# Two of eight products with B moved from VectorE to GpSimd in a state-space scan

## The chip, the cores and the metric

One NeuronCore of a Trainium2 chip runs the whole program. The metric is the device time of one execution in microseconds; of a kernel it is the median of its runs. Smaller is better. Engines are named TensorE (PE in the profile), VectorE (DVE), ScalarE (ACT), GpSimd (POOL) and SyncE (SP, which here only issues DMAs).

## The reference

The program is four layers on an image of 2 x 128 x 64 x 64 in fp32. The change touches the first layer only, two Mamba blocks over 4096 tokens of 128 channels. Cut to the recurrence:

```python
xz = x @ in_w.T
u, z = jnp.split(xz, 2, axis=-1)                 # 256 inner channels each
u = silu(causal_conv4(u) + conv_b)
dt, Bm, Cm = jnp.split(u @ xproj_w.T, [R, R + N], axis=-1)   # R = 8, N = 16
dt = softplus(dt @ dt_w.T + dt_b)
dA = exp(dt[..., None] * A)                      # token x 256 x 16
dBu = (dt * u)[..., None] * Bm[:, :, None, :]    # the product with B
def step(h, inp):                                # over the tokens
    dA_t, dBu_t, C_t = inp
    h = dA_t * h + dBu_t
    return h, einsum('bdn,bn->bd', h, C_t)       # the product with C, summed over n
y = (ys + u * ssm_D) * silu(z)                   # the gate
return y @ out_w.T                               # the mixer's output product
```

Around each block stand a layer norm, a residual, and a feed-forward part with a GELU. Layers 2 to 4 (two attentions over the image and a multi-scale attention) follow unchanged.

## The kernel before

**Chunks and steps.** The tokens go in 32 chunks of 512 (2 images x 2 blocks x 8). A chunk has 256 channels x 16 states = 4096 recurrences. They are done in eight steps, numbered 0 to 7: one step takes 32 channels and all 16 states as 128 partitions (4 groups of states, q, times 32 channels) by 4 states in the free dimension, a tile h of 128 x 4 x 512. For each step:

- `spread_dt` (line 373): four DMAs on SP copy 32 rows of dt into the four quarters of the tile dtb. `decay` (391): ScalarE takes exp(dt A) from dtb into da, a PSUM tile, four times a step.
- `spread_dtu` (380): a matmul with a selection matrix repeats 32 rows of dt * u four times down the partitions, into the PSUM tile pdu. There is one such buffer (pool l0bc), so the next spread waits until VectorE has read the last.
- `times_b` (385): VectorE multiplies bb (B, repeated down the partitions by DMA) with pdu, broadcast over the 4 states, into h. h is a ring of five buffers, taken in turn; the hidden layer of the feed-forward part, hid (452), takes one of the ring per chunk too.
- `scan` (398): VectorE runs four scans in place on h. After the fourth, GpSimd copies the last column into carry (409) and multiplies h by cb, that is C (410).
- `y_pair` (412): TensorE sums two steps over the states into py, 8 products, and so frees two h buffers.

**Order.** The order is written out by hand (`tc.manual_schedule`). Every engine works through its own queue in the order in which the program issues. A chunk has 32 slots, one for each scan; `slot` (542) issues in slot 4s: `spread_dt` for three steps ahead, `spread_dtu` for the next step, and in every second step the `y_pair` of the steps three and two before; then a scan and a decay; in slot 4s + 3 `times_b` for the next step; then what `background` (489) lists for the slot. That list holds the work of neighbouring chunks: for the next chunk n the input product (`pu_taps`, slots 0 to 5), `xproj`, `dtproj`, `soft_plus` and `dt_end` (13 to 18, the last a product on GpSimd giving dtu); for the chunk before, p, `y_out` and `gate` (slot 7; the gate is a product on GpSimd, line 433), `mix_out` on TensorE (slot 9, line 439), which reads the gated z; for p and r = i + 2 the layer norms (slots 12 to 29, with two small products on GpSimd, lines 274 and 279); for q = i - 2 the rest of the feed-forward part.

**The start.** Before chunk 0 the weights of layer 2's convolutions are folded by VectorE (`fold`, 190, slots 8 to 10 of the period -1), in raw, ulo and uhi tiles that live in the h ring, and written to DRAM from SP at once.

Of the kernel before, what the change touches and what calls it, by code (L numbers as in the profile page):

```python
# [6 lines left out]
F32 = mybir.dt.float32  # L7
AF = mybir.ActivationFunctionType
ALU = mybir.AluOpType
# [4 lines left out]
B, C, H, W = 2, 128, 64, 64  # L14
N = H * W
P = 128
CH = 512
# [50 lines left out]
def tile_conv_seq(ctx: ExitStack, tc, x, consts, vecs, wemb, wlay, wconv, wdt, wqkv, wsmall, wms, out):  # L68
    nc = tc.nc
# [46 lines left out]
    with tc.manual_schedule(), ExitStack() as s:  # L116
# [4 lines left out]
        sp = scans.enter_context(tc.tile_pool(name="l0s", bufs=1, side="right"))  # L121
        bc = scans.enter_context(tc.tile_pool(name="l0bc", bufs=1, space=PSUM, side="right"))
# [15 lines left out]
        def four(g):  # L138
            return fsel[:, g].rearrange("p q d -> p (q d)")
# [30 lines left out]
                nc.vector.tensor_tensor(u[:, k, :], cw[:, KC, :], cw[:, k, :], ALU.mult)  # L170
            wu.append(u), am.append(a)

        raws = []

        def load_rest():
            for which in range(3):
# [13 lines left out]
        def fold(which):  # L190

            g = [raws[which][:, :, k, :] for k in range(3)]
            lo, hi = (sp.tile([P, 3, 3, C], F32, name=n, tag="h", bufs=5) for n in ("ulo", "uhi"))
            tt, ts, stt = nc.vector.tensor_tensor, nc.vector.tensor_scalar, nc.vector.scalar_tensor_tensor
            tt(lo[:, 1], g[0], g[2], ALU.add)
            ts(lo[:, 1], lo[:, 1], -1.0 / 6, None, ALU.mult)
            stt(lo[:, 0], g[1], 1.0 / 6, lo[:, 1], ALU.mult, ALU.add)
            stt(lo[:, 1], g[1], -1.0 / 6, lo[:, 1], ALU.mult, ALU.add)
            stt(hi[:, 0], g[2], 4.0, g[0], ALU.mult, ALU.add)
            ts(hi[:, 0], hi[:, 0], 1.0 / 24, None, ALU.mult)  # L200
            stt(lo[:, 2], g[1], -1.0 / 12, hi[:, 0], ALU.mult, ALU.add)
            stt(hi[:, 0], g[1], 1.0 / 12, hi[:, 0], ALU.mult, ALU.add)
            ts(hi[:, 1], g[0], 0.25, None, ALU.mult)
            nc.vector.tensor_copy(hi[:, 2], g[2])
            for k, u in enumerate((lo, hi)):
                nc.sync.dma_start(ufold[which][:, 9 * k : 9 * k + 9, :], u.rearrange("p s y c -> p (s y) c"))


# [4 lines left out]
        NI, NST, NSL = len(items), 8, 32  # L213
        st = [{} for _ in items]
# [3 lines left out]
        def has(i):  # L218
            return 0 <= i < NI
# [153 lines left out]
        def spread_dt(g):  # L373
            i, s_ = divmod(g, NST)
            o = st[i]["dtb", s_] = sp.tile([P, CH], F32, name="dtb", tag="dtb", bufs=4)
            k = 32 * (s_ % 4)
            for q in range(4):
                nc.sync.dma_start(o[32 * q : 32 * q + 32, :], st[i]["dt"][k : k + 32, s_ // 4, :])

        def spread_dtu(g):  # L380
            i, s_ = divmod(g, NST)
            pdu = st[i]["pdu", s_] = bc.tile([P, CH], F32, name="pdu", tag="bc")
            nc.tensor.matmul(pdu, lhsT=four(s_ % 4), rhs=st[i]["dtu"][:, s_ // 4, :], start=True, stop=True)  # L383

        def times_b(g):
            i, s_ = divmod(g, NST)
            h = st[i]["h", s_] = sp.tile([P, 4, CH], F32, name="h", tag="h", bufs=5)
            pdu = st[i].pop(("pdu", s_))
            nc.vector.tensor_tensor(h, st[i]["bc", 0], pdu.unsqueeze(1).to_broadcast([P, 4, CH]), ALU.mult)  # L389
# [8 lines left out]
        def scan(t):  # L398
            g, m = divmod(t, 4)
            i, s_ = divmod(g, NST)  # L400
            j, gg = divmod(s_, 4)
            b, l, c = items[i]
            if (b, l) not in carries:
                carries[b, l] = sp.tile([P, NJ, 4, 4], F32, name="carry", tag="carry", bufs=2)
                nc.gpsimd.memset(carries[b, l], 0.0)
            h, da = st[i]["h", s_], st[i].pop(("da", s_, m))
            nc.vector.tensor_tensor_scan(h[:, m, :], da, h[:, m, :], carries[b, l][:, j, gg, m : m + 1], ALU.mult, ALU.add)  # L407
            if m == 3:
                nc.gpsimd.tensor_copy(carries[b, l][:, j, gg, :].unsqueeze(2), h[:, :, CH - 1 : CH])  # L409
                nc.gpsimd.tensor_tensor(h, h, st[i]["bc", 1], ALU.mult)  # L410

        def y_pair(g):

            i, s_ = divmod(g, NST)
            j, gg = divmod(s_, 4)
            if gg == 0:
                st[i]["py", j] = yp.tile([P, CH], F32, name="py", tag="y")
            py = st[i]["py", j]
            for m in range(4):
                for k in range(2):  # L420
                    r = 32 * (gg + k)
                    nc.tensor.matmul(  # L422
                        py[r : r + 32, :], lhsT=sel, rhs=st[i]["h", s_ + k][:, m, :], start=(m == 0), stop=(m == 3),
                        tile_position=(0, r),
                    )
# [63 lines left out]
        def background(i):  # L489

            todo = [[] for _ in range(NSL)]

            def at(t, f, *a):
                todo[t].append((f, a))

            n, p, q, r = i + 1, i - 1, i - 2, i + 2
            if has(q):
                at(3, gelu, q)
                at(6, ffn_down, q, (0, 1)), at(7, ffn_down, q, (2, 3)), at(9, ffn_add, q)
                at(11, out_mm, q), at(12, out_add, q)  # L500
            if has(p):
                at(7, y_out, p, 1), at(7, gate, p)
                at(9, mix_out, p), at(11, mix_add, p)
            if has(n):
                at(0, pu_taps, n, 0, (0, 1)), at(1, pu_taps, n, 0, (2, 3)), at(2, pu_out, n, 0)
                at(3, pu_taps, n, 1, (0, 1)), at(4, pu_taps, n, 1, (2, 3)), at(5, pu_out, n, 1)
                at(13, xproj, n), at(14, xproj_out, n), at(14, spread_bc, n, 0), at(22, spread_bc, n, 1)
                at(15, dtproj, n, 0), at(16, dtproj, n, 1), at(17, soft_plus, n), at(18, dt_end, n)
            if has(i):
                at(1, pz_mm, i, 0), at(3, pz_out, i, 0)  # L510
                at(5, pz_mm, i, 1), at(6, pz_out, i, 1)
            if has(i) or has(n):
                at(11, silu, i, n)
            if i == -1:
                at(1, load_rest), at(7, prepare, 1)
                for k in range(3):
                    at(8 + k, fold, k)
                at(19, spread_dtu, 0), at(26, times_b, 0)
            pair = [(k, second) for k, second in ((p, True), (r, False)) if has(k)]
            if has(r):  # L520
                at(10, embed, r), at(11, embed_out, r)
            w, m = {}, len(pair)
            for k, (it, second) in enumerate(pair):
                at(12 + 2 * k, ln_centre, w, k, it)
                at(13 + 2 * k, ln_square, w, k, it)
                at(27, ln_spread, w, k, m), at(28, ln_scale, w, k, it)
                at(29, ln_shift, w, k, it, second)
            if pair:
                at(17, ln_var, w, m), at(18, ln_eps, w, m), at(19, ln_rs, w, m), at(20, ln_newton, w, m), at(21, ln_step, w, m)
            if has(p):  # L530
                for f in range(4):
                    at(30 + f // 2, ffn_up, p, f)
            if has(i):
                at(24, y_out, i, 0)
            return todo
# [5 lines left out]
        NG, NT = NI * NST, NI * NSL  # L541
        def slot(i, todo, t_):
            t = i * NSL + t_
            g, m = divmod(t, 4)
            if m == 0 and 0 <= g + 3 < NG:
                spread_dt(g + 3)
            if m == 0 and 1 <= g + 1 < NG:
                spread_dtu(g + 1)
            if m == 0 and g % 2 == 1 and 0 <= g - 3 < NG:
                y_pair(g - 3)  # L550
            if 0 <= t < NT:
                scan(t)
            if 0 <= t + 4 < NT:
                decay(t + 4)
            if m == 3 and 1 <= g + 1 < NG:
                times_b(g + 1)
            for f, a in todo[t_]:
                f(*a)
        for i in range(-2, NI):
            todo = background(i)  # L560
            for t_ in range(NSL):
                slot(i, todo, t_)
        todo = background(NI)
        for t_ in range(8):
            slot(NI, todo, t_)
# [331 lines left out]
        sp = s.enter_context(tc.tile_pool(name="ats", bufs=1, reuse_waits="tile"))  # L897
        psa = s.enter_context(tc.tile_pool(name="atpa", bufs=2, reuse_waits="tile", space=PSUM))
        psm = s.enter_context(tc.tile_pool(name="atpm", bufs=1, reuse_waits="tile", space=PSUM))
        for now in range(NALL + LAG + 10):  # L900
            r, u = divmod(now, NU)
# [71 lines left out]
    with ExitStack() as s, tc.manual_schedule():  # L973
        sp = s.enter_context(tc.tile_pool(name="mss", bufs=1, reuse_waits="tile"))
# [60 lines left out]
        st = [{} for _ in items]  # L1035
# [433 lines left out]
```

## Time and profile before

| | |
|---|---|
| median of 3 runs | 5001.07 us (5000.54 to 5005.86) |
| the profiled execution's own time | 5004.69 us |
| its span in the trace | 5002.9 us |
| scan stage | about the first 2,100 us of the span |
| VectorE busy, of 200 us from 1000 to 1200 | 182.16 us |
| TensorE busy, same stretch | 182.66 us |
| GpSimd busy, same stretch | 139.03 us |
| products with B on VectorE | 256, mean 2272 ns |
| products with C on GpSimd | 256, mean 4535 ns |
| spreads of dtu on TensorE | 256 products, 512 matmul records |

The profile gives busy time per engine, groups of equal instructions (line, engine, operation, output <- inputs, count, then busy us, mean ns, idle before them and what ended it), and a timeline. A timeline line has the start and the length in us, the engine, the line, the instruction, how many are merged, and in brackets the idle time before it with its releaser. An fp32 matmul leaves two records; L383 is a line of the kernel. SPq is the DMA queue of SP. All times count from the span's start.

### The profile page before, as it was taken

The numbers are of one execution on the slowest core, as the hardware profiler recorded it, in microseconds if no ns is written. First come the engines' busy times: TensorE is split into PE (matmuls) and PEld (weight loads), VectorE is DVE, ScalarE is ACT, GpSimd is POOL, SyncE is SP. The second block draws the span as 40 slices with busy tenths as digits, with TensorE's granted clock in tenths as the row PEclk, the third lists the DMA queues.
The fourth block names the chain that finished last, engine by engine and source line by source line (L and its number), as shares of the span: only waits on it lengthen the run. The fifth ranks groups of instructions, "written<-read, shape, count | busy, mean of one in ns | idle before, by whom it ended". The sixth has DMA issues, their size and how long they took to land. (4 is left out here: it accounts for less than half of the span.)

```text
span 5002.9 us, 48954 instructions
## 1 busy us (share of the span) xinstructions
PE 4661.3 (93%) x14797; PEld 2242.4 (45%) x14797; DVE 4024.6 (80%) x4283; ACT 2358.8 (47%) x3218; POOL 2337.5 (47%) x1974
## 2 busy tenths in 40 slices
PE   5889999999988899899999999999999999999997
PEld 1222222222222222366667766666666666333332
DVE  6999999999999999878886677767776775667776
ACT  4677777777777777522222222233333332323332
POOL 3777776766777777513332133333333332333331
PEclk8898889989999989899999999999999999999998
DMA  6333333322323333214444344434443443000000
GB/s 163 69 68 68 69 71 70 69 65 62 72 67 68 70 73 73 73 53 113 109 110 123 105 112 111 120 95 114 110 100 98 112 113 88 3 7 7 5 7 9
DMA packets 242343, 386.24 MB, mean 77 GB/s; under 512 B 88592, under 2 KB 88992, under 8 KB 233632
## 3 DMA queue, kind: packets, MB, share of 16 engines
q1 hardware_dynamic: 192928, 315.94, 26.0%
q10 hardware_dynamic: 49152, 67.17, 5.4%
q8 instruction: 118, 1.93, 0.2%
q14 instruction: 145, 1.19, 0.1%
HBM read 101.02 MB, written 13.37 MB: 23 GB/s over the span
## 5 line engine op out<-in xcount | busy, mean ns | idle before, releaser
L792 POOL COPY pt<-tr 32x512 f32<-32x512 f32 x1024 | 650.8, 636 | 1437.3 <-DVE tr L785 704.7
L407 DVE TENSOR_TENSOR_SCAN h<-da,carry,h 128x512 f32<-128x512 f32 x1024 | 1241.6, 1266 | 59.7 <-ACT da L396 30.7
L410 POOL TENSOR_TENSOR h<-h,cb 128x2048 f32<-128x2048 f32 x256 | 1160.9, 4535 | 21.0 <-POOL carry L409 0.4
L755 PE MATMUL pq<-k,q 128*128 128x512 f32 x2048 | 962.6, 593 | 7.0 <-DVE sc L760 7.0
L805 PE MATMUL po<-pt,vt 128*128 128x256 f32 x4096 | 965.7, 379 | 2.5 <-DMA pt<-tr 2.5
L770 ACT ACTIVATE sc<-sc,nm 128x2048 f32<-128x2048 f32 x256 | 510.6, 1995 | 912.8 <-DVE nm L766 701.6
L805 PEld LDWEIGHTS po<-pt,vt 128*128 128x128 f32 x4096 | 777.9, 190 | 294.8 <-issue 208.3
L760 DVE TENSOR_SCALAR_CACHE_REDUCE sc<-pq 128x1024 f32<-128x1024 f32 x512 | 625.1, 1222 | 315.6 <-PE pq L755 294.3
L396 ACT ACTIVATE da<-dtb,am 128x512 f32<-128x512 f32 x1024 | 681.5, 684 | 230.5 <-DVE h L407 207.9
L389 DVE TENSOR_TENSOR h<-bb,pdu 128x2048 f32<-128x2048 f32 x256 | 581.7, 2272 | 86.0 <-PE py L422 29.3
L785 DVE STREAM_TRANSPOSE tr<-sc 128x2048 f32<-128x2048 f32 x256 | 591.6, 2311 | 64.6 <-DMA pt<-tr 56.2
L422 PE MATMUL py<-h,sel 128*32 128x512 f32 x2048 | 511.0, 643 | 1.6 <-POOL h L410 1.6
L755 PEld LDWEIGHTS pq<-k,q 128*128 128x128 f32 x2048 | 382.9, 190 | 283.2 <-issue 247.2
L383 PE MATMUL pdu<-dtu,fsel 128*128 128x512 f32 x512 | 325.3, 721 | 117.0 <-DVE h L389 114.8
L422 PEld LDWEIGHTS py<-h,sel 128*32 128x32 f32 x2048 | 115.2, 117 | 415.0 <-issue 409.5
L310 PE MATMUL pu<-xn,wu 128*128 128x512 f32 x512 | 246.2, 614 | 2.6 <-ACT xn L300 1.7
L383 PEld LDWEIGHTS pdu<-dtu,fsel 128*128 128x128 f32 x512 | 95.9, 214 | 322.0 <-DVE h L389 199.5
L409 POOL COPY carry<-h 128x4 f32<-128x4 f32 x256 | 47.8, 187 | 394.5 <-DVE h L407 392.7
L1219 DVE TENSOR_TENSOR ov<-v,pw 128x2048 f32<-128x2048 f32 x64 | 146.2, 2285 | 62.1 <-PE pw L1212 62.1
L1153 PE MATMUL pqkv<-f,ws 128*128 128x512 f32 x384 | 188.2, 615 | 3.0 <-DVE prod L1170 2.3
L1223 POOL TENSOR_TENSOR ov<-ov 128x2048 f32<-128x2048 f32 x16 | 72.6, 4538 | 235.5 <-DVE ov L1219 235.5
L370 POOL TENSOR_TENSOR dtu<-dt,u 128x1024 f32<-128x1024 f32 x32 | 75.1, 2348 | 192.6 <-ACT dt L364 192.6
(259 smaller groups left out, 5266.6 us busy)
## 6 DMA issues: line engine op xcount, KB each, us to landing
pt<-tr SPq DMA_DIRECT2D x2048, 64.0 KB, 2.0
dtb<-dt SPq DMA_DIRECT2D x1024, 64.0 KB, 2.0
pt<-tr ACTq DMA_DIRECT2D x1024, 64.0 KB, 2.2
bb<-dr SPq DMA_DIRECT2D x128, 256.0 KB, 4.4
cb<-dr SPq DMA_DIRECT2D x128, 256.0 KB, 4.6
uw<-ufold SPq DMA_DIRECT2D x12, 576.0 KB, 4.3
uw<-dkept SPq DMA_DIRECT2D x20, 288.0 KB, 3.0
xt<-in_x SPq DMA_DIRECT2D x16, 256.0 KB, 4.6
```

What stands on the lines that cost most here:

```text
L383: nc.tensor.matmul(pdu, lhsT=four(s_ % 4), rhs=st[i]["dtu"][:, s_ // 4, :], start=True, stop=True)
L389: nc.vector.tensor_tensor(h, st[i]["bc", 0], pdu.unsqueeze(1).to_broadcast([P, 4, CH]), ALU.mult)
L396: nc.scalar.activation(da, st[i]["dtb", s_], AF.Exp, scale=am[items[i][1]][:, j, gg, m : m + 1])
L407: nc.vector.tensor_tensor_scan(h[:, m, :], da, h[:, m, :], carries[b, l][:, j, gg, m : m + 1], ALU.mult, ALU.add)
L410: nc.gpsimd.tensor_tensor(h, h, st[i]["bc", 1], ALU.mult)
L422: nc.tensor.matmul(py[r : r + 32, :], lhsT=sel, rhs=st[i]["h", s_ + k][:, m, :], start=(m == 0), stop=(m == 3), tile_position=(0, r),)
L755: nc.tensor.matmul(pq[:, i, :], lhsT=sta["q", r, grp][:, it * P : (it + 1) * P], rhs=sta["k"][:, at : at + CH], start=True, stop=True)
L760: nc.vector.tensor_scalar(dst, pq, 1.0, None, ALU.mult, ALU.max, accum_out=sta["mx"][:, c2 : c2 + 1])
L770: nc.scalar.activation(sc, sc, AF.Exp, bias=nm, scale=scale, accum_out=sm[:, hh : hh + 1])
L785: nc.vector.transpose(tr, sta.pop(("sc", r, blk, hh)).rearrange("p (t r f) -> p r t f", r=NB, f=32))
L792: nc.gpsimd.tensor_copy(dst, src)
L805: nc.tensor.matmul(sta["po", r, grp], lhsT=sta["vt"][:, jt, :], rhs=rhs, start=(jt == 0), stop=(jt == N // P - 1))
```

## The change

In every chunk, steps 3 and 5 (the fourth and the sixth) are taken out of `spread_dtu` and `times_b`. Instead SP copies their rows of dtu into an SBUF tile dub with four DMAs (`spread_pool`, in slots 0 and 5; dub has one buffer), and GpSimd makes the product with B from dub and bb (`times_b_pool`, in slots 4 and 11). The h tiles of these steps are so taken from the ring earlier than before, in the order 1, 3, 2, 5, 4, 6, 7, hid, 0. So that the folding at the start fits the ring, the folded tiles of one of the three convolutions go into the buffers of bb and cb, and the writes to DRAM are issued in slot 23 instead of slots 8 to 10.

```diff
-        raws = []
+        raws, folded = [], []
...
         def fold(which):
             g = [raws[which][:, :, k, :] for k in range(3)]
-            lo, hi = (sp.tile([P, 3, 3, C], F32, name=n, tag="h", bufs=5) for n in ("ulo", "uhi"))
+            tags = (("h", 5), ("h", 5)) if which != 1 else (("bb", 2), ("cb", 2))
+            lo, hi = (sp.tile([P, 3, 3, C], F32, name=n, tag=t, bufs=k) for n, (t, k) in zip(("ulo", "uhi"), tags))
+            folded.append((lo, hi))
...
-            for k, u in enumerate((lo, hi)):
+
+        def fold_out(which):
+            for k, u in enumerate(folded[which]):
                 nc.sync.dma_start(ufold[which][:, 9 * k : 9 * k + 9, :], u.rearrange("p s y c -> p (s y) c"))
...
+        BY_POOL = (3, 5)
+
+        def spread_pool(i, s_):
+            o = st[i]["dub", s_] = sp.tile([P, CH], F32, name="dub", tag="dub")
+            k = 32 * (s_ % 4)
+            for q in range(4):
+                nc.sync.dma_start(o[32 * q : 32 * q + 32, :], st[i]["dtu"][k : k + 32, s_ // 4, :])
+
+        def times_b_pool(i, s_):
+            h = st[i]["h", s_] = sp.tile([P, 4, CH], F32, name="h", tag="h", bufs=5)
+            dub = st[i].pop(("dub", s_))
+            nc.gpsimd.tensor_tensor(h, st[i]["bc", 0], dub.unsqueeze(1).to_broadcast([P, 4, CH]), ALU.mult)
...
             if has(i):
+                at(0, spread_pool, i, 3), at(4, times_b_pool, i, 3)
+                at(5, spread_pool, i, 5), at(11, times_b_pool, i, 5)
...
                 for k in range(3):
-                    at(8 + k, fold, k)
+                    at(8 + k, fold, k), at(23, fold_out, k)
...
-            if m == 0 and 1 <= g + 1 < NG:
+            if m == 0 and 1 <= g + 1 < NG and (g + 1) % NST not in BY_POOL:
                 spread_dtu(g + 1)
...
-            if m == 3 and 1 <= g + 1 < NG:
+            if m == 3 and 1 <= g + 1 < NG and (g + 1) % NST not in BY_POOL:
                 times_b(g + 1)
```

## Prediction

> **What bounds the kernel now.** I read the page's table of engines first, then the costliest groups, then one chunk of the scan stage as a timeline of each engine. The change touches only the scan stage, the first 2,100 us of the span.
>
> ```profile
> PE 4661.3 (93%) x14797; PEld 2242.4 (45%) x14797; DVE 4024.6 (80%) x4283; ACT 2358.8 (47%) x3218; POOL 2337.5 (47%) x1974
> ...
> L389 DVE TENSOR_TENSOR h<-bb,pdu 128x2048 f32<-128x2048 f32 x256 | 581.7, 2272 | 86.0 <-PE py L422 29.3
> ```
>
> One product with B costs VectorE 2.27 us; one product with C (line 410), of the same shape, costs GpSimd a mean of 4535 ns. The stage looks VectorE-bound: by the table of stretches it is busy 182 to 189 of every 200 us, TensorE 179 to 183, GpSimd 139 to 145. Two engines are near their limit, so the order of one chunk decides. A chunk takes 62 to 63 us. TensorE in one of them (start, length, instruction, wait before it):
>
> ```profile
> 442.16 4.40 PE L422 MATMUL py<-h,sel 128*32 128x512 f32 x16
> ...
> 458.22 3.63 PE L422 MATMUL py<-h,sel 128*32 128x512 f32 x16
> ...
> 468.94 1.02 PE L383 MATMUL pdu<-dtu,fsel 128*128 128x512 f32 x2
> 469.80 1.88 PE L439 MATMUL po<-z,wl 128*128 128x512 f32 x4
> ...
> 482.29 1.13 PE L383 MATMUL pdu<-dtu,fsel 128*128 128x512 f32 x2
> 483.34 1.12 PE L358 MATMUL pt<-dbl,wd 8*128 8x512 f32 x2
> 486.01 3.57 PE L258 MATMUL var<-sq,kc 128*2 128x512 f32 x4 [1.54 <-ACT dt L364]
> 489.51 2.08 PE L383 MATMUL pdu<-dtu,fsel 128*128 128x512 f32 x2
> ...
> 502.17 2.08 PE L383 MATMUL pdu<-dtu,fsel 128*128 128x512 f32 x2 [2.54 <-DVE h L389]
> ```
>
> From 442 to 484 no wait is shown: TensorE works solidly. I number the steps 0 to 7 as the code does. 442.16 is the state sum (py) of steps 4 and 5 of the chunk before, 458.22 that of steps 6 and 7, 468.94 and 482.29 the spreads for steps 3 and 5 (those that go), 469.80 the mixer's output product (mix_out), 489.51 the spread for step 6. VectorE and GpSimd meanwhile:
>
> ```profile
> 461.95 2.29 DVE L389 TENSOR_TENSOR h<-bb,pdu 128x2048 f32<-128x2048 f32 x1 [1.00 <-PE py L422]
> ...
> 492.10 2.26 DVE L389 TENSOR_TENSOR h<-bb,pdu 128x2048 f32<-128x2048 f32 x1
> ```
>
> ```profile
> 454.19 4.55 POOL L410 TENSOR_TENSOR h<-h,cb 128x2048 f32<-128x2048 f32 x1
> 461.01 0.19 POOL L409 COPY carry<-h 128x4 f32<-128x4 f32 x1 [2.28 <-DVE h L407]
> 461.28 4.54 POOL L410 TENSOR_TENSOR h<-h,cb 128x2048 f32<-128x2048 f32 x1
> 465.78 2.36 POOL L433 TENSOR_TENSOR z<-z,u 128x1024 f32<-128x1024 f32 x1
> ```
>
> Step 2's product waits at 461.95 for the state sum of 6 and 7, because it takes over a buffer of the h ring. Step 6's product at 492.10 comes 0.6 us after its spread (489.51 + 2.08): TensorE and VectorE arrive there nearly together. On GpSimd, 461.28 is step 1's product with C, and 465.78 is the gate. The gate ends at 468.14, and mix_out, which reads it, starts at 469.80: 1.7 us of room.
>
> **What the Trainium skill says.** "GPSIMD Engine Reference", section 3.1, prices a two-input product of N=2048 in fp32 at 4497 ns on GpSimd and 2293 ns on VectorE; the trace has 4535 and 2272, so it agrees. Sections 1 and 8 of that page say that the two engines share SBUF interfaces and contend when VectorE has two SBUF inputs. In this stage da and pdu lie in PSUM, and the trace shows none: four scans take 4.81 us at 449.04, where GpSimd stands for more than half of them (from 451.2 to 453.9), and 4.80 at 464.81, where it works until 468.1. "TensorE: Matmul & The Clock Gate", Part 1, says that an idle window of about 3.4 us halves the array's clock and that a busy one restores it. The trace agrees: granted clock 0.50 from 499 to 502, and the spread after 2.54 us of idle takes 2.08 instead of 1.02.
>
> **The change part by part.** (a) *Off VectorE:* 64 products x 2.27 = 145 us. All of it would be gain only if VectorE ended last. (b) *Off TensorE:* the spreads at 468.94 (0.86 us to the next start) and 482.29 (1.05). (c) *Onto GpSimd:* 64 x 4.54 = 290 us. Per chunk it has 45 us of work; it gets 54. That is under 62, so throughput holds; what matters is where the products stand in its in-order queue.
>
> Step 3's product stands after step 0's product with C and ahead of step 1's, and the gate comes next. It takes the ring's buffer of the previous step 6 (the ring now turns 0, 1, 3, 2, 5, 4, 6, 7, hid, with five buffers), so it waits for the state sum that ends at 461.85. Step 0's product with C ends at 458.74, so GpSimd stands 3.1 us. Then: step 3's product to 466.4; carry copy and step 1's product with C (0.27 + 4.54) to 471.2; gate (2.36) to 473.6. TensorE, one spread shorter, would reach mix_out at 468.94: it stands 4.7 us, and mix_out starts 3.8 us later than before. Behind mix_out on TensorE are the spread for step 4, the state sum of 0 and 1, the LN centring, xproj, dtproj, the variance and the spread for step 6. Less the 1.05 of the spread for step 5, that last one comes 2.75 us later, ending at 494.3 instead of 491.6.
>
> Does VectorE absorb it? Step 4's product now takes step 0's buffer (before: that of hid) and so waits for the state sum of 0 and 1, at 480.9; with its 2.39 and two steps of scans (2 x 4.73) VectorE is ready for step 6 at 492.7, and waits for the spread. Step 6's product moves from 492.10 to 494.4: +2.3. From there to the next chunk the path is VectorE alone (two products, scans, y_out), the spread at 502.17 and the state sum. So +2.3 to +2.75 per chunk; I take 2.5. The other chunks carry the two output matmuls after mix_out, which moves nothing in this argument.
>
> (d) *The clock.* The new stop of 4.7 us is longer than those of 1.5 and 2.5 us after which the trace already shows half clock. Half clock for 3.4 us after restart costs 1.7 us; the stretches of the trace run 3.4 to about 6 us after a restart, so 1.7 to 2.9, or nothing if the stop meets no window. I take 1.9. Sum: +4.4 per chunk, in 30 of the 32 (1 to 30, where the gate and the next chunk's projections both exist): +132.
>
> (e) *GpSimd's later work.* Step 5's product ends at 482.9, needed at 488; step 3's product with C at 487.7, needed at 494.3; dtu waits for ScalarE until about 489.4. All hidden; the nearest cover (TensorE's own delay) is 1.7 us for dtu, and where it goes, up to 1 us per chunk.
>
> (f) *SP.* Per chunk 8 more DMAs of 64 KB, some 5 us of issue at the 0.64 us of the dtb rows (SP's own timeline: 2.50 for four). dub has one buffer: step 5's copies wait on SP until GpSimd ends step 3's product at 466.4, and dtb for step 5 is queued behind; ScalarE needs that about 483. Nothing to pay; if that cover were gone, 2 us.
>
> (g) *The start.*
>
> ```profile
> 70.49 2.29 DVE L389 TENSOR_TENSOR h<-bb,pdu 128x2048 f32<-128x2048 f32 x1 [10.28 <-DMA bb<-dr]
> ```
>
> ```profile
> 60.24 0.32 SPq L206 DMA_DIRECT2D ufold<-uhi  x1
> 60.65 0.40 SPq L349 DMA_DIRECT2D dr<-dbl  x1
> ```
>
> dr stood behind the folded weights on SP, though dbl was there at 47.9. With fold_out later, step 0 can begin when VectorE ends folding, at 60.2: up to -10.3. But now six 576 KB writes precede dtb for step 1, whose scans take part of it back: 0 to -10.3, taken -5. Chunk 0 has no gate: -4 (of 2 x 2.27). Chunk 31, without projections, +2.
>
> Sum: 132 - 5 - 4 + 2 = +125. The profiled execution took 5004.69 us (span 5002.9, 1.8 around it), 3.6 above the median of 5001.07; against the median, **5126 us**.
>
> **Rivals.** *Slower, without the clock:* 30 x 2.5 - 7 = +68, 5069. *Much slower:* half clock lasts 2.9 us' worth and (e) loses its cover: 30 x (2.75 + 2.9 + 1) - 7 = +192, 5193. *Faster:* VectorE ends last. Place: mix_out; price: the 4.7 us stop; it decides for a gain as soon as GpSimd's gate is done by about 470, i.e. if step 3's product need not wait for the state sum of 6 and 7 (it would end at 463.3 and the gate at 470.5). Then TensorE's two spreads less are worth 1.6 per chunk: 30 x -1.6 - 7 = -55, 4946; if TensorE had slack everywhere, -145 - 7, 4849. For it speaks VectorE's busy share, the largest; against it TensorE's 42 us without a wait and the room of only 1.7 us. *Same:* the change does not act: not possible, the products do move; but a stop of half the size cancels with the start, 5001.
>
> **How the numbers follow.** Forecast 0.56, slower without the clock 0.18 (together 5035 to 5175: 30 x 1.4 to 30 x 5.7 a stage, less 7), much slower 0.10, same 0.05, faster 0.11. The range, 5035 to 5190, leaves out faster, same and about 0.04 at the top. About 0.2% is what a measurement of this kernel can tell from no change. Slower 0.84, same 0.05, faster 0.11.
>
> **What would show it.** After: idle of TensorE before mix_out, released by GpSimd's gate, 4 to 5 us a chunk; step 3's product waiting for py; half clock just after; step 6's product on VectorE waiting for the spread; VectorE's busy time down 145 us; chunks of 66 to 67 us. Wrong if mix_out shows no wait or chunks take 60 us.

## The result, and the profile after

The changed kernel takes a median of 5170.61 us (5166.73 to 5174.97, four runs) against 5000.81 for the kernel before in the same series: a ratio of 1.0333, with an interval of 1.0320 to 1.0345. It is slower by 169.8 us, 45 more than the forecast of 5126, inside the range. The profiled execution took 5169.39 us, its span is 5167.6; against the one of before (5004.69) that is +164.7. All of it lies in the scan stage. From the gate of one chunk to that of the next there pass 62.95 us before and 68.41 after, in 31 intervals: 31 x 5.46 = +169.4 (30 of them are longer by 5.67 on the mean, the last is 0.8 shorter). The first gate comes 6.9 us earlier (142.72 against 149.60), what follows the last one takes 2.2 more: 169.4 - 6.9 + 2.2 = 164.7.

The page of the kernel after, the table of engines and three groups (busy us, mean ns, idle before and its main releaser):

```profile
PE 4668.3 (90%) x14669; PEld 2240.1 (43%) x14669; DVE 3876.2 (75%) x4219; ACT 2359.5 (46%) x3218; POOL 2623.6 (51%) x2038
...
L407 DVE TENSOR_TENSOR h<-bb,pdu 128x2048 f32<-128x2048 f32 x192 | 436.4, 2273 | 351.5 <-PE py L440 332.3
...
L401 POOL TENSOR_TENSOR h<-bb,dub 128x2048 f32<-128x2048 f32 x64 | 297.9, 4654 | 98.8 <-PE py L440 92.7
L457 PE MATMUL po<-z,wl 128*128 128x512 f32 x128 | 108.9, 1000 | 145.7 <-POOL z L451 145.7
```

VectorE lost 148 us of work, GpSimd gained 286, and neither figure explains the time. The idle columns do. Before, the products with B on VectorE had 86 us of idle ahead of them; now the 192 that are left have 351.5, nearly all of it for the state sum py. And mix_out (L457), which waited for the gate only once before, for 3.9 us at the start, has 145.7 us ahead of it for the gate z on GpSimd: 29 waits of 4.53 to 4.57 us, 7.2 in the first chunk and 6.5 near the end. The granted clock fell from 0.950 to 0.934 as a mean of the whole span.

TensorE in one chunk of the kernel after:

```profile
472.66 3.63 PE L440 MATMUL py<-h,sel 128*32 128x512 f32 x16
...
482.51 1.02 PE L487 MATMUL pf<-xt,kc 128*128 128x512 f32 x2
488.10 2.99 PE L457 MATMUL po<-z,wl 128*128 128x512 f32 x4 [4.56 <-POOL z L451]
490.88 1.76 PE L458 MATMUL po<-xt,kc 128*128 128x512 f32 x2
...
506.11 3.51 PE L262 MATMUL var<-sq,kc 128*2 128x512 f32 x4 [2.08 <-ACT dt L368]
509.55 1.12 PE L387 MATMUL pdu<-dtu,fsel 128*128 128x512 f32 x2
```

GpSimd in the same stretch:

```profile
468.62 4.55 POOL L428 TENSOR_TENSOR h<-h,cb 128x2048 f32<-128x2048 f32 x1
476.36 4.66 POOL L401 TENSOR_TENSOR h<-bb,dub 128x2048 f32<-128x2048 f32 x1 [3.19 <-PE py L440]
480.96 0.20 POOL L427 COPY carry<-h 128x4 f32<-128x4 f32 x1
481.24 4.51 POOL L428 TENSOR_TENSOR h<-h,cb 128x2048 f32<-128x2048 f32 x1
485.70 2.34 POOL L451 TENSOR_TENSOR z<-z,u 128x1024 f32<-128x1024 f32 x1
```

This is the chain that the prediction wrote out. GpSimd stands 3.19 us, because step 3's product needs the h buffer that the state sum (472.66 to 476.29) frees. Then come that product, the product with C of step 1, and the gate, which ends at 488.04. TensorE has been ready since 483.5, stands 4.56 us, and starts again at half clock: the four matmuls of mix_out take 2.99 us here and 3.78 in many other chunks, where they took 1.88, and L458 takes 1.76 instead of 1.02.

VectorE, with what stands between:

```profile
479.29 9.50 DVE L425 TENSOR_TENSOR_SCAN h<-da,carry,h 128x512 f32<-128x512 f32 x8
497.08 2.29 DVE L407 TENSOR_TENSOR h<-bb,pdu 128x2048 f32<-128x2048 f32 x1 [8.29 <-PE py L440]
...
508.67 1.28 DVE L425 TENSOR_TENSOR_SCAN h<-da,carry,h 128x512 f32<-128x512 f32 x1 [2.03 <-ACT da L414]
510.94 1.28 DVE L425 TENSOR_TENSOR_SCAN h<-da,carry,h 128x512 f32<-128x512 f32 x1 [0.99 <-ACT da L414]
512.14 2.26 DVE L407 TENSOR_TENSOR h<-bb,pdu 128x2048 f32<-128x2048 f32 x1
```

Step 4's product (497.08) waits 8.29 us for the state sum of steps 0 and 1, which is queued on TensorE behind mix_out. That looks like the loss, but it isn't where the chunk is decided: VectorE is soon held up again, at 508.67 and 510.94, by ScalarE's decays, and step 6's product at 512.14 follows the last scan without a wait for its own spread (ready at 510.67).

To see which stretch grew I cut each chunk at three marks, as a mean over 29 chunks of each trace (without the first and the last two, where neighbouring chunks are missing): the start of the state sum of steps 6 and 7, the start of mix_out, and step 6's product on VectorE.

| | state sum to mix_out | mix_out to step 6's product | step 6's product to next state sum | chunk |
|---|---|---|---|---|
| before | 11.58 | 22.42 | 29.31 | 63.31 |
| after | 15.43 | 24.99 | 28.52 | 68.95 |
| difference | +3.85 | +2.57 | -0.79 | +5.64 |

### The profile page after: what moved, and what is told of

Its sections match the earlier page's. It is cut to its first block, busy times and chain, and to the rows that moved or that the text cites. A ratio compares the mean times of both kernels' runs of the same rounds, so it can differ in the third digit from the quotient of the medians.

```text
span 5167.6 us, 49020 instructions
## 1 busy us (share of the span) xinstructions
PE 4668.3 (90%) x14669; PEld 2240.1 (43%) x14669; DVE 3876.2 (75%) x4219; ACT 2359.5 (46%) x3218; POOL 2623.6 (51%) x2038
## 4 chain that ended last, share of the span: by engine, by line
PE 56%; DVE 15%; POOL 9%; ACT 6%; DMA 5%; issue 4%; SPq 3%; ACTq 0%; DVEq 0%; POOLq 0%
PE po L825 11%; PE pq L775 10%; PE py L440 6%; DVE tr L805 4%; DMA pt<-tr 4%; POOL h L428 4%; POOL h L401 4%; DVE h L425 3%; SPq L816 3%; PE pu L314 3%; PE pdu L387 2%; PE pa L672 2%; DVE h L407 2%; PE ph L473 2%; PE pf L1146 2%
## 5 line engine op out<-in xcount | busy, mean ns | idle before, releaser
L428 POOL TENSOR_TENSOR h<-h,cb 128x2048 f32<-128x2048 f32 x256 | 1158.9, 4527 | 21.0 <-PE pz L327 0.4
L407 DVE TENSOR_TENSOR h<-bb,pdu 128x2048 f32<-128x2048 f32 x192 | 436.4, 2273 | 351.5 <-PE py L440 332.3
L387 PE MATMUL pdu<-dtu,fsel 128*128 128x512 f32 x384 | 256.2, 755 | 111.9 <-DVE h L407 109.6
L401 POOL TENSOR_TENSOR h<-bb,dub 128x2048 f32<-128x2048 f32 x64 | 297.9, 4654 | 98.8 <-PE py L440 92.7
L457 PE MATMUL po<-z,wl 128*128 128x512 f32 x128 | 108.9, 1000 | 145.7 <-POOL z L451 145.7
L387 PEld LDWEIGHTS pdu<-dtu,fsel 128*128 128x128 f32 x384 | 76.1, 225 | 273.7 <-DVE h L407 171.9
L1243 POOL TENSOR_TENSOR ov<-ov 128x2048 f32<-128x2048 f32 x16 | 72.6, 4535 | 237.2 <-DVE ov L1239 237.2
```

The source lines that it names most:

```text
L401: nc.gpsimd.tensor_tensor(h, st[i]["bc", 0], dub.unsqueeze(1).to_broadcast([P, 4, CH]), ALU.mult)
```

## The experiments

All ratios are against the kernel before, run on the same chip beside it, with 95% intervals; "after" stands at 1.0333. No experiment leaves out part of the computation; two add matmuls whose results nobody reads.

**Which of the two steps, or neither?** Three kernels were run beside each other. `only3` leaves step 5 where it was:

```diff
-        BY_POOL = (3, 5)
+        BY_POOL = (3,)
-                at(5, spread_pool, i, 5), at(11, times_b_pool, i, 5)
```

> Only step 3's product is on GpSimd; step 5's is back on VectorE, its spread back on TensorE. Queue theory (step 3's product holds the gate back, the gate holds mix_out, and ScalarE's and TensorE's queues stand behind mix_out): mix_out still waits about 4.6 us for the gate in every chunk and nearly the whole loss stays: 5130 to 5180 us. Ring theory (what hurts is step 4's product on VectorE waiting for the state sum of steps 0 and 1, whose buffer it takes over): here step 4 takes the buffer of hid again, so the wait of 8 us and the loss go: 4940 to 5000. Load theory (GpSimd has too much work): about half the loss, 5085.

`only5` is the mirror image:

```diff
-        BY_POOL = (3, 5)
+        BY_POOL = (5,)
-                at(0, spread_pool, i, 3), at(4, times_b_pool, i, 3)
```

> Only step 5's product is on GpSimd, behind the gate in its queue. Queue theory: no wait before mix_out, no loss; little gain either, because step 6's product already waited for the decays of ScalarE and the spread: 4960 to 5000 us, of it some 12 from the earlier start. Ring theory: step 4 still takes the buffer of step 0 and the loss stays: 5080 or more. Load theory: about half the loss, 5085.

`start_only` has BY_POOL = () and neither line, so only the change to the folding at the start is left:

> No product on GpSimd; only the folded weights are written to DRAM later and lie in other buffers. All theories: the start is about 12.5 us earlier (step 0's product at 58.0 instead of 70.5 us), of which the late dtb may take some back: 4989 us, between 4986 and 5001.

Measured: only3 5169.08 us, 1.0327 (1.0311 to 1.0342); only5 4999.08, 0.9988 (0.9981 to 0.9994); start_only 4996.31, 0.9982 (0.9974 to 0.9990). The whole loss comes from step 3's product. Step 5's costs at most a few us (the intervals of only5 and start_only overlap), and it gains nothing either, though it takes 72 us off VectorE: VectorE does not end last by as much as one product. Much of what it gains its scans spend waiting for ScalarE's decays (49.0 us between 400 and 1600, against 18.3 in start_only). The waits of only3 between 400 and 1600 us (us in total, times, longest):

```profile
ACT xt L461 <- PE po L458: 128.7, 17, 8.2
DVE h L407 <- PE pdu L387: 114.0, 25, 8.3
...
PE po L457 <- POOL z L451: 82.0, 18, 4.6
```

The third line is to the digit that of the kernel after. The second shows what became of the wait of 8.29 us: in only3 the ring turns otherwise, step 4 does not wait for py, and it waits as long for its spread pdu, which stands behind mix_out in the same queue. So the buffer that step 4 takes in the ring's new order is no cause by itself; who is named as releaser depends on what happens to stand last behind the late mix_out. (That step 3's product has to wait 3.19 us for its own buffer remains a link of the chain.)

**Is it ScalarE's queue behind mix_out?** ScalarE takes mix_out's result (L461) and has the SiLU of the next chunk queued behind it. `silu_first` issues the SiLU one slot earlier, ahead of that copy:

```diff
-                at(11, silu, i, n)
+                at(10, silu, i, n)
```

> As the changed kernel, but the SiLU with its two table loads (4.6 us) is issued to ScalarE in slot 10, ahead of the copy that waits for mix_out. If ScalarE's queue behind mix_out ends last (step 6's product waits for the scans of step 5, these for the decays), the chunk gets shorter until TensorE's own delay shows, by 1.0 to 1.5 us: 5125 to 5140 us. If TensorE's spread for step 6 ends last, as the prediction had it, nothing changes: 5165 to 5175.

It took 5171.96 us, 1.0335 (1.0318 to 1.0352), inside the range that the expectation kept for TensorE's spread ending last. The trace does not show that. In the same 29 chunks the spread is ready 0.5 to 1.5 us before step 6's product, and in 28 of them that product follows a scan that waited for a decay. But with the SiLU ahead of the copy, ScalarE waits for the next thing that TensorE makes behind mix_out, the layer norm's centring pc:

```profile
496.36 0.60 ACT L255 ACTIVATE sq<-pc 128x512 f32<-128x512 f32 x1 [3.69 <-PE pc L248]
```

(65.8 us in 17 such waits between 400 and 1600 us, against 2.1 in the kernel after.) So the delay reaches ScalarE by a second way, and little could be won. That even this little is lost may be the half clock: mix_out takes more than 3.7 us in 20 of 30 chunks, against 13 in the kernel after. warm_silu below tests it.

**Is it the gate behind step 3's product?** `gate_first` issues step 3's product behind the gate:

```diff
-                at(0, spread_pool, i, 3), at(4, times_b_pool, i, 3)
+                at(0, spread_pool, i, 3), at(8, times_b_pool, i, 3)
```

> Both products stay on GpSimd, but step 3's is issued in slot 8, behind step 1's product with C and the gate, instead of slot 4. Queue theory: the gate ends where it did in the kernel before, mix_out no longer waits, the loss goes; step 3's scans wait about 3 us for their product instead, which step 4's product and the scans behind it can absorb: 4980 to 5015 us. Load theory (GpSimd's 54 us of work per chunk): the loss stays, since the work is the same: above 5085.

5130.11 us, 1.0249 (1.0234 to 1.0265): about a quarter of the loss went, a miss by over 100 us, in the range that load theory had named. The wait at mix_out is gone all the same, and the chunks without the layer's output product take 63.1 us on the mean, 62.8 before. The others, with that product (L499, L500), take 73.5, 64.0 before. There TensorE waits for something else:

```profile
787.55 1.02 PE L499 MATMUL po<-xt,we 128*128 128x512 f32 x2
797.30 2.07 PE L500 MATMUL po<-xr,kc 128*128 128x512 f32 x2 [8.73 <-DMA xr<-in_x]
```

SP of gate_first, in the same stretch:

```profile
788.79 2.41 SPq L396 DMA_DIRECT2D dub<-dtu  x4
791.30 2.43 SPq L382 DMA_DIRECT2D dtb<-dt  x4
793.83 0.53 SPq L493 DMA_DIRECT2D xr<-in_x  x1
```

xr is the block's input for the residual. Its load is queued on SP behind step 5's copies into dub, and those can only be issued once GpSimd has read step 3's rows out of the single dub buffer. In gate_first GpSimd reads them until 788.77, and the copies start at 788.79. In the kernel after, mix_out is itself late and hides this: no wait for xr is seen there, and between 400 and 1600 us none of its computing engines waits for any DMA. So the trace gives a second buffer alone nothing to win there; it was not run.

`gate_dub2` takes that away too, with a second buffer:

```diff
-                at(0, spread_pool, i, 3), at(4, times_b_pool, i, 3)
+                at(0, spread_pool, i, 3), at(8, times_b_pool, i, 3)
-            o = st[i]["dub", s_] = sp.tile([P, CH], F32, name="dub", tag="dub")
+            o = st[i]["dub", s_] = sp.tile([P, CH], F32, name="dub", tag="dub", bufs=2)
```

> As gate_first, with two buffers for dub instead of one. In gate_first the chunks with an output product took 73 us and the others 63.2; in the long ones TensorE waited 8.7 us for the DMA of xr, which stands on SP behind step 5's copies into dub, and these wait for GpSimd to end step 3's product. SP theory: with two buffers the copies need not wait, all chunks take about 63, and the time is 4990 to 5010 us, within 0.3% of before. If the long chunks have another cause: 5130 as before.

4982.42 us, 0.9961 (0.9947 to 0.9975): the loss is gone, and the time is 8 us below the range expected. Both products still stand on GpSimd, which rules out load theory, and the kernel is faster than the one before. (Part of that is the earlier start: start_only alone stands at 0.9982.) So the cause is where step 3's product stands in the queue, not that GpSimd makes it, and the single buffer is a second trap behind it.

**How much is the half clock?** `warm` leaves the gate late and fills the stop with five matmuls whose result is not read:

```diff
+        def warm(i):
+            pw = mmt("warm")
+            for k in range(5):
+                nc.tensor.matmul(pw, lhsT=ident, rhs=kc[:, :CH], start=(k == 0), stop=(k == 4))
-                at(9, mix_out, p), at(11, mix_add, p)
+                at(8, warm, p), at(9, mix_out, p), at(11, mix_add, p)
```

> As the changed kernel, with five extra matmuls on constants (some 4.3 us, into a PSUM tile that nobody reads) on TensorE just ahead of mix_out, in the place where it stood still. Clock theory: the half clock after the stop costs 1.8 us of mix_out's 3.7 us delay turned 5.6, so it goes: 68.4 us a chunk become 66.6, 5115 us (5100 to 5130). If the loop of a chunk is locked to the windows of the clock (chunks in the changed kernel keep near 68.3, in two experiments that took away different things), it jumps by a whole 3.4 us or not at all: 5065 or 5170. If the clock plays no part, 5170.

```profile
477.86 4.45 PE L456 MATMUL warm<-kc 128*128 128x512 f32 x10
482.58 1.98 PE L462 MATMUL po<-z,wl 128*128 128x512 f32 x4 [0.27 <-POOL z L451]
484.41 1.02 PE L463 MATMUL po<-xt,kc 128*128 128x512 f32 x2
```

5129.51 us, 1.0248 (1.0232 to 1.0263). TensorE is given more to do, the program is 41 us faster, and mix_out is back at 1.98 us (1.88 before). In the three marks: 15.45, 23.03, 28.93, chunk 67.41. The middle stretch gives back 2.0 of its 2.6; the first keeps its +3.9. The half clock is worth 41 / 30 = 1.4 us a chunk by the times, 1.5 by the marks, and some 4.1 us a chunk are lost with no half clock at mix_out at all.

`warm_silu` is warm with the edit of silu_first:

> The changed kernel with both the five extra matmuls of warm and the earlier SiLU of silu_first. silu_first brought step 6's product 1.2 us a chunk nearer to mix_out, and yet nothing was gained; its mix_out and its state sum of 4 and 5 ran longer at half clock. If the half clock ate it: without the half clock at mix_out the earlier SiLU is worth up to 1.2 us a chunk, 5090 to 5120 us against 5130 for warm. If ScalarE's queue does not decide at all: 5125 to 5135.

5113.85 us, 1.0220 (1.0203 to 1.0237), 16 below warm (the intervals of the two ratios just overlap), and 58 below silu_first: the same early SiLU that gave nothing at half clock gives some 0.5 us a chunk without it. ScalarE now spends the stop on the SiLU (its wait ahead of the copy of mix_out's result, L466 here, falls from 99.6 us in warm to 14.7 in the window of 400 to 1600), but then it waits 69.5 us for the centring pc (1.9 in warm), the scans wait for its decays (88.0 us, 47.8 in warm), and most of the delay stays.

**Can mix_out simply come later?** `mix_late` moves mix_out and its copy behind the state sum that VectorE waits for, to slot 12, and with them the layer norm's first two parts:

```diff
-                at(9, mix_out, p), at(11, mix_add, p)
+                at(12, mix_out, p), at(12, mix_add, p)
-                at(12 + 2 * k, ln_centre, w, k, it)
-                at(13 + 2 * k, ln_square, w, k, it)
+                at(13 if second else 14, ln_centre, w, k, it)
+                at(14 if second else 15, ln_square, w, k, it)
```

> Both products stay as in the changed kernel, but mix_out and its copy are issued in slot 12, behind the spread for step 4 and the state sum of steps 0 and 1, and the layer norm's centring of that chunk one slot later. Queue theory: TensorE waits only for step 1's product with C, about 2 us, and not for the gate; step 4's product on VectorE no longer stands behind it: most of the loss goes, 4950 to 5030 us. If GpSimd's load or the ring were the cause: above 5085.

5094.44 us, 1.0177 (1.0160 to 1.0194), a miss by 64 us, in the range kept for GpSimd's load or the ring. Two waits of 400 to 1600 us say more:

```profile
DVE h L425 <- ACT da L414: 106.7, 106, 2.7
...
PE po L500 <- DMA xr<-in_x: 30.3, 8, 4.2
```

The second is the dub buffer again, and it is most of what is left: the chunks with the output product take 70.1 us on the mean, 64.0 before, the others only 63.6, 62.8 before. The first is ScalarE: the decays now stand behind a later copy and layer norm in its queue, and the scans wait for them 106 times, against 37 in the kernel after.

**A better version.** In all these kernels the variance product of the layer norm (var) waits on TensorE for ScalarE's softplus, with step 6's spread behind it, and ScalarE's last decay of step 5 stands behind `ve`, which waits for var. `only5_var` takes only5 and puts these five operations later:

```diff
-                at(17, ln_var, w, m), at(18, ln_eps, w, m), at(19, ln_rs, w, m), at(20, ln_newton, w, m), at(21, ln_step, w, m)
+                at(20, ln_var, w, m), at(20, ln_eps, w, m), at(20, ln_rs, w, m), at(21, ln_newton, w, m), at(22, ln_step, w, m)
```

> Only step 5's product on GpSimd, and the layer norm's variance on TensorE moved from slot 17 to slot 20, behind the spread for step 6 and the state sum of 2 and 3 (its further steps to slots 20 to 22). If step 6's product waits for that spread behind the variance, which waits for ScalarE, VectorE's room of 2.3 us per chunk becomes usable: 4930 to 4960 us. If the decays behind the softplus on ScalarE end last, or the layer norm becomes late instead: 4985 to 5010.

4955.69 us, 0.9898 (0.9883 to 0.9913). `gate_dub2_var`, the same edit on gate_dub2:

> As gate_dub2, with the layer norm's variance moved to slot 20 as in only5_var. If GpSimd's second product can be used at all, it is now no worse than only5_var: 4930 to 4960 us. If the 3 us that step 3's scans wait for their product eat what it frees: 4955 to 4990.

4948.59 us, 0.9895 (0.9880 to 0.9910). `start_var`, the same edit on start_only, with all products on VectorE:

> No product on GpSimd, the start as in start_only, and the variance in slot 20 as in only5_var. It tells whether the gain of only5_var comes from the product that left VectorE or from the variance alone. If VectorE had no room before (its step 6 was ready when the spread was), the variance alone gives little: 4980 to 5000 us. If TensorE alone was late: 4950 to 4960, as only5_var.

5033.28 us, 1.0063 (1.0048 to 1.0078), slower than before: a miss for the expectation on either side. Its trace shows what the later layer norm costs, from 400 to 1600 us:

```profile
PE pr L287 <- POOL rs L283: 90.0, 19, 5.3
```

(35.6 us, longest 2.7, in start_only; 49.8, longest 2.7, in only5_var.) So the move of var gains 0.9% with step 5's product off VectorE (4955.69 against 4999.08) and loses 0.7% without (5033.28 against 4996.31). That VectorE's freed time is what pays for it is the plainest reading, not shown; the step in between was not followed in the trace. Both best versions beat the kernel before by 1.0%; their intervals do not tell them apart.

## Why the prediction was right, and where a term was off

**The cause** was right in each link: the wait for the ring's buffer (predicted 3.1 us, measured 3.19), the gate queued behind step 3's product, the stop at mix_out (4.7, measured 4.56), mix_out later by 3.8 (measured +3.85), half clock after it. One sign that it named did not come: step 6's product on VectorE does not wait for its spread, but follows scans that wait for ScalarE. only3 and gate_dub2 show that this product at this place in the queue makes the loss.

**The mis-sized term is the "+2.3 to +2.75 per chunk; I take 2.5".** Without the clock the chunk loses 67.41 - 63.31 = 4.1 us (warm), not 2.5. The step that failed is "Less the 1.05 of the spread for step 5, that last one comes 2.75 later", with VectorE's slack on top: 3.8 us of delay became 2.5 before they reached step 6's product. The credit did not come because another chain ends last there. The prediction saw the spread and VectorE arrive "nearly together" (0.5 us apart, not 0.6) and followed TensorE. ScalarE before, the copy of mix_out's result and the last two steps ahead of step 6:

```profile
472.57 0.59 ACT L443 COPY xt<-po 128x512 f32<-128x512 f32 x1 [1.55 <-PE po L440]
...
489.62 0.68 ACT L262 ACTIVATE ve<-var,eps 2x512 f32<-2x512 f32 x1 [1.08 <-PE var L258]
490.20 0.67 ACT L396 ACTIVATE da<-dtb,am 128x512 f32<-128x512 f32 x1
```

and after:

```profile
492.67 0.59 ACT L461 COPY xt<-po 128x512 f32<-128x512 f32 x1 [7.22 <-PE po L458]
...
509.65 0.68 ACT L266 ACTIVATE ve<-var,eps 2x512 f32<-2x512 f32 x1 [1.02 <-PE var L262]
510.24 0.67 ACT L414 ACTIVATE da<-dtb,am 128x512 f32<-128x512 f32 x1
```

From the copy to the end of the last decay it takes 18.3 us before and 18.2 after: ScalarE's queue (copy, SiLU, decays, softplus, ve, decay) moved as a block. Before as well as after, the scan that waits for this decay is followed at once by step 6's product (492.10, 512.14); that is so in 16 of the 29 chunks before and in 28 after. Nor did the missing spread speed up TensorE: var waits for the softplus, 2.08 us instead of the 1.54 before. So the 3.8 us arrive whole, and on top of them the 1.8 us that the copy itself comes later after mix_out (4.57 instead of 2.77), at half clock: 5.6 up to step 6's product of this chunk. (As a mean it is 6.4 up to there, and the rest of the chunk gives 0.8 back.) This link is read from the traces of before and after. warm_silu supports it with 0.5 us, and there the delay comes to ScalarE through the centring pc instead; no run took ScalarE's whole queue out of the way.

In the sum, the chunks cost 30 x 5.67 = 170 instead of 132. This term alone is 38 of the 40 us by which the profiled executions (+164.7) miss the +125.

**The clock (d).** Taken 1.9, measured 1.4 in the times and 1.5 in the marks (warm). "TensorE: Matmul & The Clock Gate", Part 1, of the Trainium skill, says that an idle window of about 3.4 us halves the clock. The trace agrees: after stops of 4.53 to 4.57 us mix_out took 2.99 to 3.78 us in all eight chunks from 480 to 1000 us, where 1.88 is its length without a stop. But the trace before shows half clock without such a stop too: the granted clock is 0.50 there from 498.4 us on, with TensorE at work until 499.6, so the stop of 2.54 us that the prediction quotes came after it and, by these records, did not bring it on. What did is not shown. The two errors work against each other: 4.1 + 1.5 = 5.6 against 4.4 forecast. That the forecast came as near as it did is in part this luck.

**GpSimd's later work (e)** was right: step 5's product costs nothing that can be told apart (only5 against start_only). The price is a little higher, 4654 ns a product with B against 4535 assumed: 0.1 us each. (The 4497 ns that the prediction quotes are the skill page's figure for an add.)

**SP (f).** "Nothing to pay" holds in the kernel after, but the wrong transfer was named. The prediction saw dtb behind the copies into dub and overlooked xr, two places further on. Once mix_out is early, TensorE waits 7.4 to 9.4 us for xr in 14 chunks (gate_first), not 2; it made gate_first miss.

**The start (g).** Step 0's product begins at 58.01 instead of 70.49, -12.5, more than the bound of -10.3. At the first gate, which comes after chunk 0, -6.9 are left, where -5 for the start and -4 for chunk 0 were taken. start_only keeps -11.4 at its first gate and is faster than before by 0.18%, so it is the moved products that take 4.5 back in chunk 0 instead of giving 4: there step 3's product waits 6.1 us for its copies into dub, and scans wait for decays, spreads and state sums.

**The rivals.** *Faster* named its own turning point: a gate not held up by step 3's product. gate_dub2 does that (and frees dub), and comes to 4982, faster as this rival said, though not its 4946. *Slower without the clock* is 5069 by the prediction and 5129.5 in warm, mostly because it had the same wrong credit (30 x 1.6 = 48 us). *Much slower*, 5193, is by its size the nearest of all, but for other reasons: (e)'s cover held, and the half clock cost less than it assumed. One sum does not come out: 30 x 5.7 less 7 is 164, so forecast and *slower without the clock* together end at 5165, not 5175, and the measured 5170.6 lies just above them.

## What to carry to other kernels

Work moved to an engine with time to spare lands in an in-order queue: look first at what stands behind it there, and who waits for that. A credit may be taken only on the chain that really ends last, and where two engines arrive "nearly together" both have to be followed back, with the third one that feeds them. A one-buffer tile filled from a DMA queue can hold up every later transfer in that queue, and here that stayed hidden until the first delay was mended.

## What the runs showed of the hardware

- Matmuls that do nothing made the program faster: 320 records of them, 4.45 us in each stop, for -41 us.
- The granted clock changes in these records in whole steps of 3.413 us. In the kernel after, 10 of the 31 intervals from gate to gate last 68.2 to 68.5 us and three 71.5 to 71.6, near 20 and 21 such steps, but the others (but for the last, of 50.0) lie between 67.5 and 70.6, and warm has nine chunks of 68.2 or 68.3 with no half clock at mix_out. A loop locked to these steps would have put warm at 5065 or 5170; it took 5129.5. So a lock is not shown, and why silu_first gained nothing stays open in part.
- The product with B from two SBUF inputs, one of them broadcast over the states, takes GpSimd 4654 ns against 4527 for the product with C; it takes 4625 in gate_first, where only the place of step 3's differs, and 4592 in gate_dub2.
- At the start, VectorE's folding product of two SBUF inputs took 1.78 us beside a GpSimd product in the kernel after and 2.47 before, where the same product takes 0.55 with GpSimd idle; the scans and products of the stage, which have one operand in PSUM, show nothing of the kind beside GpSimd.
- Not tried: two dub buffers in the changed kernel as it stands, and mix_late with two dub buffers.
